# Base weights staged in the attention's operand room, under a newly planned order of instructions: a four-layer block on one core

## The chip, the cores and the metric

The kernel runs on one core of a Trainium2 chip. The metric is the device time of one execution in microseconds, as a median over several runs. The core has five engines that each take their instructions strictly in order: PE (matmul), DVE (vector), ACT (activation), POOL (general purpose), and SP, which issues all DMA transfers of this kernel.

## The reference

The input is x, 32 batches of 128 positions x 1024 channels in float32, and a context of the same shape. Four layers follow each other, each added to its input after a layer norm:

```
x = x + autocorrelation(norm(x), ctx, ctx)     # 8 heads; circular correlation by FFT over the 128
                                               # positions, top 9 lags per channel, softmax, gather
x = x + lora_moe(norm(x), W_base, ...)         # 1024x1024 base product + 8 experts of rank 16, top 2
x = x + windowed_attention(norm(x), ctx, ...)  # channels = the 128 rows, T = 1024, 8 heads, window 16
x = x + lora_moe4(norm(x), A, B, Wr)           # 4 experts of rank 16, top 2
```

The batches are independent of each other.

## The kernel before

Each batch is a 128 x 1024 tile in two halves of 512 columns. `load_batch` loads ctx and x (four DMAs of 256 KB) and splits the scaled ctx into two f16 pieces (high and low; products of two such pairs are taken as three f16 matmuls, `three`). `autocorr` works on one half: `spectrum` multiplies ctx by Fourier matrices and completes the result by two small SBUF-to-SBUF copies on SP (`u<-u`), `cross` multiplies spectra, the stage "top" finds nine lags on DVE, "wt" turns the weights, "inv" goes back. `ffn0` is the base product with its gate, `attention` the windowed attention, `ffn1` the last layer, whose input is turned by DMA transposes (`turn`).

In `attention`, the queries of one half are spread block-diagonally over `qbd` (8 DMAs, one for each head) and the values, written to DRAM (`vd`) before, over `vbd` (4 DMAs). Each is a fixed SBUF tile of 16 KB per partition; only its diagonal blocks are written, so the rest has to be zero from the start. Both are zeroed in the set-up by one POOL memset each (`keep`, L470 and L471).

All other large values live in 49 general slots, `u`, of 128 x 512 float32 each. `prep_ffn` (L542, stage "ws") prepares the weights once: it loads the base weights by 16 DMAs of 256 KB into 16 `u` slots (L552 to L557), takes their largest absolute value on DVE (`wmx`), and after the scale is known makes two f16 pieces of each (`wsp`) on ACT with DVE or POOL; only then the slots are free.

The order of all instructions is worked out on the host before the kernel is emitted. `Planner` records every operation with an estimated duration (`_cost`) and simulates the five engines: whenever one is free it takes, of the operations that are ready, the one with the lowest priority number, if its slots can be had.

```
prio = lambda o: (period * max(o.batch, 0) - o.tail - bias.get(o.stage, 0.0) - bias.get(o.stage + "/" + o.eng, 0.0), o.index)
```

Here `o.tail` is the longest chain of work behind the operation within its batch, `period` is the configuration's T, and the biases (in us) are set for each stage and each stage on an engine. `win` limits how many batches are in flight; `margin`, `su`, `sp`, `ru` and `rp` rule when an operation must leave slots to older ones. `phases` is a list of such sets, each valid from the simulated time `at`. The last entry of `slack` is added to every DMA's duration after the set-up. For a DMA, `op.dur` is the time to landing and `op.cold` how long it occupies SP. The emitted program follows this order on each engine; the trace therefore gives L364 (the emitting line) for almost all instructions, and groups are told apart by their tiles.

Of the kernel before, what the change touches and what calls it, by code (L numbers as in the profile page):

```python
# [12 lines left out]
F32 = mybir.dt.float32  # L13
F32R = mybir.dt.float32r
F16 = mybir.dt.float16
# [7 lines left out]
S = 128  # L23
D = 1024
HALF = 512
EPS = 1e-5
NEG = -3.0e38
TINY = 1e-30
CFG = {'nu': 49, 'en': 'G', 'cl': 'G', 'xl': 'G', 'sm': 'V', 'sw': 'A', 'wg': 'VG', 'q0': 'G', 'ns': 28, 'nt': 48, 'plan': {'phases': [{'at': 0.0, 'T': 20.35, 'margin': 52, 'win': 6, 'su': 75, 'sp': 99, 'ru': 1, 'rp': 0, 'bias': {'kv': -28.7, 'load': 5.3, 'S': -3.8, 'gate': 75.2, 'ffn1': 5.8, 'q': -6.6, 'top': 0.3, 'PV': 0.0, 'inv': 4.8, 'wt': 98.4, 'spec': 6.9, 'wo': 95.5, 'ws': -11.6, 'base': 1.1, 'ffn0': 85.5, 'corr': 4.1, 'setup': -12.4, 'S/Pool': 23.1, 'kv/PE': -6.8, 'kv/Pool': 1.8, 'gate/Activation': -32.5, 'ffn1/Pool': 15.3, 'q/DVE': 34.4, 'q/Activation': 38.2, 'q/Pool': 8.2, 'ffn0/Pool': 52.9, 'setup/PE': -21.7, 'corr/Pool': -8.1, 'gate/DVE': -34.8, 'setup/SP': 26.1, 'corr/Activation': -7.8, 'corr/PE': 3.9, 'wo/DVE': -60.5, 'setup/DVE': 3.5, 'wt/DVE': 1.1, 'load/SP': -11.1, 'spec/SP': -32.0, 'base/DVE': -1.8, 'ws/Activation': -3.7, 'load/PE': 12.0, 'inv/DVE': 3.1, 'load/Activation': -1.9, 'load/Pool': -12.1, 'ws/Pool': -68.6, 'gate/PE': 6.2, 'ws/SP': -23.3, 'PV/Activation': 35.6, 'ffn1/PE': -3.5, 'ws/PE': -45.6, 'inv/Pool': 4.0, 'corr/DVE': 7.5, 'ffn1/SP': 70.1, 'setup/Pool': -26.5, 'top/DVE': 6.4, 'setup/Activation': -2.6, 'top/Pool': 106.8, 'ffn1/Activation': 35.0, 'spec/Activation': 16.1, 'wt/Activation': 35.3, 'ffn0/PE': 3.2, 'q/SP': 5.5, 'q/PE': 0.6, 'ffn0/Activation': -36.7, 'ws/DVE': 17.5, 'top/Activation': 22.8, 'ffn0/DVE': -21.6, 'inv/Activation': 3.1, 'load/DVE': 8.9, 'ffn1/DVE': 62.8, 'inv/PE': 0.0, 'wo/PE': -38.0, 'PV/DVE': 46.6, 'PV/PE': -2.9, 'S/Activation': 6.7, 'wt/PE': 28.9, 'kv/DVE': 19.9, 'S/DVE': 2.0, 'kv/Activation': -7.2, 'kv/SP': 29.4, 'S/PE': -0.3, 'base/PE': -0.9, 'spec/PE': 0.3, 'PV/Pool': 49.6}}], 'slack': [1.0, 0, 292.364]}}
NTOP = int(2 * math.log(S))  # L30
X_SC = 2.0 ** 10
W_SC = 2.0 ** 14
# [72 lines left out]
class Planner:  # L105
# [72 lines left out]
    def _cost(self, op, method, v, kw):  # L178
        size = lambda x: int(np.prod(x.shape[1:]))
        eng, out = op.eng, v["out"]  # L180
        n = size(out)
        src = next((v[k] for k in ("in_", "in0", "1", "in_values") if k in v), out)
        psum = any(x.proto.space == PSUM for x in v.values())
        nsc = sum(tuple(x.shape[1:]) == (1,) for k, x in v.items() if k in ("scale", "bias", "scalar", "scalar1", "scalar2", "2", "3"))
        if eng == "PE":
            rhs = v["rhs"] if "rhs" in v else v["2"]
            n = size(rhs)
            if method == "transpose":
                warm, cold, cols = 107.0, 213.0, 256.0
            elif rhs.proto.dtype == F32:  # L190
                warm, cold, cols = max(222.0 if n > 64 else 140.0, n / 0.6 + 10), max(214.0, n / 0.3), 4.0 * n
            else:
                warm, cold, cols = max(24.8, n / 2.4 + 2.5), max(26.7, n / 1.2), n
                if rhs.proto.dtype == F32R:
                    warm, cold = max(107.0, warm), max(214.0, cold)
            op.dur += warm
            op.cold += cold
            op.cols += cols * src.shape[0] / 128
            return
        if eng == "Activation":  # L200
            op.dur += (n + (61 if src.proto.space == PSUM else 112)) / 1.2 + 94 * (nsc + ("accum_out" in v))
            if src.region()[0] != out.region()[0]:
                op.dur += 127.0
            elif out.proto.ap[-1][0] > 1:
                op.dur += 0.2 * n
        elif eng == "DVE":
            n = max(n, size(src))
            two = method in ("tensor_copy", "tensor_scalar", "memset") and not psum and n > 64
            op.dur += 6 * n / 0.96 + 67 if method == "reciprocal" else (n * (0.5 if two else 1.0) + 64 + 59 * nsc) / 0.96
            op.dur += 70.0 * ("accum_out" in v) + {"match_replace": 67.0, "transpose": 25.0}.get(method, 0.0)  # L210
        elif eng == "Pool":
            small = mybir.dt.size(out.proto.dtype) == 2
            if method == "memset":
                op.dur += 40.0 + (0.85 if small else 0.2) * n
            else:
                rate = (2.8 if small else 1.2) if method == "tensor_scalar" else 1.88 if small else 2.1
                if any(x.proto.ap[-1][0] == 0 for x in v.values()) and n > 128:
                    rate = 1.67
                op.dur += 530.0 if kw.get("op") == ALU.pow else 150.0 + rate * n
        else:  # L220
            run = out.proto.ap[-1][1] * mybir.dt.size(out.proto.dtype)
            dram = any(x.tile is None for x in v.values())
            op.dur += (3200.0 if dram else 2900.0 if run > 128 else 3500.0) + out.shape[0] * n * mybir.dt.size(out.proto.dtype) / 360.0

            op.cold = 450.0 if dram else 720.0 if run > 128 else 840.0
            if kw.get("transpose"):
                op.dur, op.cold = 4400.0, 1430.0

# [147 lines left out]
def mk_kernel(ctx: ExitStack, tc: tile.TileContext, T: dict, out: bass.AP):  # L376
# [8 lines left out]
    def slot(name, shape, dt=F32):  # L385
        return cp.tile(shape, dt, tag=name, name=name)

    slots = {
        "u": [slot(f"u{i}", [128, HALF]) for i in range(CFG["nu"])],
        "p": [pp.tile([128, HALF], F32, tag=f"p{i}", name=f"p{i}") for i in range(8)],  # L390
        "m": [slot(f"m{i}", [128, 128]) for i in range(6)],
        "s": [slot(f"s{i}", [128, 16]) for i in range(CFG["ns"])],
        "t": [slot(f"t{i}", [128, 4]) for i in range(CFG["nt"])],
        "r": [slot(f"r{i}", [128, 128], F32R) for i in range(6)],
    }
    P = Planner(slots)
    V, A, G, PE, SP = (P.engine(n, e) for n, e in zip(
        ("DVE", "Activation", "Pool", "PE", "SP"), (nc.vector, nc.scalar, nc.gpsimd, nc.tensor, nc.sync)))

    def U():  # L400
        return P.tile("u")

    def B():
        return P.tile("p")

    def M():
        return P.tile("m")
# [52 lines left out]
    def keep(name, shape, dt, fill, eng=G):  # L460
        t = P.fixed(slot(name, shape, dt))
        eng.memset(t if dt == F32 else t.bitcast(F32), fill)
        return t
# [3 lines left out]
    tl8, tl4 = ([keep(f"tl{e}_{i}", [128, 8], F32, NEG) for i in range(2)] for e in (8, 4))  # L467
    k16 = keep("k16", [128, 2, D + 16], F16, 0.0)

    qbd = keep("qbd", [128, 2, 32, 128], F16, 0.0)  # L470
    vbd = keep("vbd", [128, 32, 128, 2], F16, 0.0)  # L471


    wst, woT, wb = U(), const("woT", [128, 128]), load("wb")
# [46 lines left out]
    for src, sc, dst in ((wq, sq, None), (wk, rsc[:, 0:1], wk16), (wv, rsc[:, 1:2], wv16)):  # L521
        t, p = M(), B()
# [19 lines left out]
    def prep_ffn():  # L542
# [3 lines left out]
        def load_ar(name, i, w, rows):  # L546
            t = U()[:, 0 : rows * w].rearrange("p (k n) -> p k n", n=w)
            SP.dma_start(out=t, in_=T[name][i * rows * 128 : (i + 1) * rows * 128].rearrange("(k p) n -> p k n", p=128))
            return t


        wb = []  # L552
        for k in range(16):
            t = U()
            SP.dma_start(out=t, in_=T["wbT"][k // 2 * 128 : (k // 2 + 1) * 128, k % 2 * HALF : (k % 2 + 1) * HALF])
            absmax(mx[:, k : k + 1], t)
            wb.append(t)  # L557
        for i in range(4):
            t = load_ar("ar8T", i, 136, 2)
            absmax(mx[:, 16 + i : 17 + i], t[:, :, 0:128], AX.XY)  # L560
            absmax(mx[:, 20 + i : 21 + i], t[:, :, 128:136], AX.XY)
        for i in range(2):
            t = load_ar("ar4T", i, 68, 4)
# [30 lines left out]
        for i in range(4):  # L594
            t = load_ar("ar8T", i, 136, 2)
            for lo, hi, c in ((0, 128, 1), (128, 136, 2)):
                pieces([wsp[:, r, 2 * i : 2 * i + 2, D + lo : D + hi] for r in range(2)], t[:, :, lo:hi], c)
        for k in range(16):
            lo = k % 2 * HALF
            pieces([wsp[:, r, k // 2, lo : lo + HALF] for r in range(2)], wb[k], 0, CFG["wg"][k % len(CFG["wg"])])  # L600
        for i in range(2):
            t = load_ar("ar4T", i, 68, 4)
            for lo, hi, c in ((0, 64, 3), (64, 68, 4)):
                pieces([ar4[:, r, 4 * i : 4 * i + 4, lo:hi] for r in range(2)], t[:, :, lo:hi], c)
        for g in range(2):
            t, sl = U(), slice(g * HALF, (g + 1) * HALF)
# [3 lines left out]
        for g in range(2):  # L610
            t, r, sl = U(), U(), slice(g * HALF, (g + 1) * HALF)
# [5 lines left out]

    prep_ffn()
    P.behind = ()


    def ln_first(src):
# [82 lines left out]
    def load_batch(b):  # L705
# [17 lines left out]
        for g in range(2):  # L723
            if CFG["cl"] == "G":
                A.activation(c16[g][:, 0], c[g], AF.Copy, scale=sc)
# [28 lines left out]
    def autocorr(b, hf, normalise, x, c16, ksc, sums):  # L754
# [3 lines left out]
        q, q16, p = normalise(hf), pair(U()), B()  # L758
        split(q16[:, 0], q16[:, 1], q, G if CFG["q0"] == "G" else V)
        three(p, wdft[:, 0], q16)  # L760
# [333 lines left out]
```

## Time and profile before

| | |
|---|---|
| median of 3 runs | 1609.07 us (1606.35 to 1609.52) |
| profiled execution | 1606.64 us, span 1604.9 us |
| mean granted PE clock | 0.966 |
| PE, DVE, ACT, POOL busy | 94%, 89%, 89%, 85% of the span |
| DMA engines, share of the span | 61.3% (queue of SP) |
| DMA traffic | 179.62 MB, mean 112 GB/s |

The times of engines overlap. Slices of the span are 40 us; in the lines quoted below, `u<-in_ctx` means that a general slot is written from the input ctx, `x` with a number counts instructions, and in square brackets stands how long the engine idled before and what released it.

### The profile page before, as it was taken

What the parts mean: (1) busy time and instruction counts of PE and PEld (TensorE: products, weight loads), DVE (VectorE), ACT (ScalarE), POOL (GpSimd) and SP (SyncE); (2) the same over time, 40 slices, a digit from 0 to 9 for tenths busy, and PEclk for the clock granted to TensorE, in tenths of its full rate; (3) what the DMA queues carried; (4) which work ended last, traced back from release to release, by engine and by line L of the source; (5) the groups of instructions that cost most, each with busy time, mean ns of one, the idle gap of its engine ahead of it and who ended that gap; (6) DMA issues with size and microseconds to landing.
All of it is one profiled execution on the core that took longest, in us unless ns stands there. A gap on an engine that the chain in (4) does not pass through costs nothing.

```text
span 1604.9 us, 52637 instructions
## 1 busy us (share of the span) xinstructions
PE 1504.2 (94%) x19469; PEld 1005.0 (63%) x19469; DVE 1420.7 (89%) x4922; ACT 1420.5 (89%) x2833; POOL 1358.0 (85%) x1569
## 2 busy tenths in 40 slices
PE   3589999999999999999999999999999999999954
PEld 1246666766676666666666666666666666766642
DVE  6878999999999999999999999999999999989753
ACT  5788999999999999999999999999999999998642
POOL 5778988998888899888888998888889988898742
PEclk7799999999999999999999999999999999999975
DMA  8325566666656666566566666657666566666562
GB/s 252 105 75 82 87 111 127 118 113 125 109 105 115 119 120 123 113 127 101 103 126 117 118 119 121 125 98 110 114 127 120 110 128 106 102 96 93 85 78 54
DMA packets 957058, 179.62 MB, mean 112 GB/s; under 512 B 877360, under 2 KB 912960, under 8 KB 956800
## 3 DMA queue, kind: packets, MB, share of 16 engines
q1 hardware_dynamic: 956800, 176.25, 61.3%
q8 instruction: 154, 2.52, 0.6%
q14 instruction: 104, 0.85, 0.2%
HBM read 75.36 MB, written 33.82 MB: 68 GB/s over the span
## 4 chain that ended last, share of the span: by engine, by line
PE 52%; ACT 25%; DVE 9%; DMA 5%; issue 5%; SPq 2%; POOL 1%; ACTq 0%; POOLq 0%; DVEq 0%
PE p L364 52%; ACT u L364 24%; DVE u L364 7%; DMA vbd<-vd 3%; SPq L364 2%; DMA u<-in_x 1%; POOL u L364 1%; ACT k L364 1%; DVE t L364 1%; DMA u<-u 1%; DMA vd<-u 0%; DVE wsp L364 0%; DMA u<-in_wbT 0%; DVE wmx L364 0%; DMA u<-in_wa 0%
## 5 line engine op out<-in xcount | busy, mean ns | idle before, releaser
L364 POOL TENSOR_TENSOR u<-u,u 128x512 f16<-128x512 f32 (+1 forms) x704 | 844.6, 1227 | 56.4 <-ACT u L364 51.7
L364 PE MATMUL p<-wsp,u 128*128 128x512 f16 (+1 forms) x2304 | 398.1, 329 | 2.6 <-ACT u L364 1.4
L364 PEld LDWEIGHTS <-u 128*128 128x128 f16 x3840 | 271.2, 99 | 187.7 <-DMA u<-u 13.6
L364 ACT ACTIVATE u<-p,t 64x512 f32<-64x512 f32 (+3 forms) x512 | 316.8, 648 | 22.2 <-PE p L364 12.4
L364 ACT ACTIVATE u<-u,t 128x512 f32<-128x512 f32 (+1 forms) x448 | 314.8, 723 | 22.7 <-DVE t L364 14.1
L364 ACT ACTIVATE u<-p 64x512 f32<-64x512 f32 (+1 forms) x512 | 299.7, 592 | 36.9 <-PE p L364 29.7
L364 DVE SCALAR_TENSOR_TENSOR u<-p,u 128x512 f32<-128x512 f32 (+1 forms) x384 | 255.6, 678 | 30.2 <-ACT u L364 19.1
L364 PE MATMUL p<-u,ch 128*128 128x512 f16 x960 | 244.3, 385 | 2.7 <-DVE u L364 1.7
L364 DVE SCALAR_TENSOR_TENSOR u<-p,t,u 128x512 f16<-128x512 f32 (+1 forms) x256 | 157.8, 626 | 63.5 <-ACT u L364 62.7
L364 ACT ACTIVATE u<-u,t,t 128x512 f32<-128x512 f32 (+1 forms) x256 | 192.8, 829 | 4.9 <-POOL t L364 3.9
L364 PEld LDWEIGHTS <-vbd 128*128 128x128 f16 x6144 | 161.8, 97 | 45.0 <-issue 44.7
L364 PEld LDWEIGHTS <-qbd 128*128 128x128 f16 x6144 | 171.0, 96 | 25.1 <-issue 1.9
L364 PE MATMUL p<-u,vbd 128*128 128x32 f16 x6144 | 165.7, 177 | 18.6 <-ACT u L364 12.1
L364 PE MATMUL p<-k,qbd 128*128 128x32 f16 x6144 | 174.7, 176 | 1.0 <-DMA vd<-u 1.0
L364 PEld LDWEIGHTS <-ch 128*128 128x128 f16 x960 | 93.0, 102 | 129.4 <-issue 52.7
L364 ACT ACTIVATE u<-u 128x512 f16<-128x512 f32 x194 | 119.5, 639 | 54.5 <-DVE u L364 54.3
L364 POOL TENSOR_TENSOR u<-u,t 128x512 f32<-128x512 f32 x64 | 65.5, 1043 | 81.0 <-DVE t L364 78.1
L364 POOL TENSOR_TENSOR u<-u,s 128x512 f32<-128x512 f32 x128 | 131.7, 1049 | 0.5
L364 PE MATMUL p<-u,cf 128*128 128x512 f32 x256 | 123.9, 604 | 1.2 <-POOL u L364 0.8
L364 POOL TENSOR_TENSOR t<-t,mhalf 128x1 f32<-128x1 f32 x128 | 72.4, 565 | 46.0 <-DVE t L364 45.6
L364 DVE STREAM_TRANSPOSE u<-u 128x512 f32<-128x512 f32 x128 | 89.8, 703 | 9.7 <-POOL u L364 9.2
L364 PE MATMUL p<-ident,u 128*128 128x128 f32 x512 | 82.2, 286 | 11.3 <-POOL u L364 5.4
(163 smaller groups left out, 2661.5 us busy)
## 6 DMA issues: line engine op xcount, KB each, us to landing
vbd<-vd SPq DMA_DIRECT2D x256, 128.0 KB
u<-u SPq DMA_DIRECT2D x192, 128.0 KB
u<-in_ctx SPq DMA_DIRECT2D x64, 256.0 KB
u<-in_x SPq DMA_DIRECT2D x64, 256.0 KB
vd<-u SPq DMA_DIRECT2D x64, 256.0 KB
qbd<-u SPq DMA_DIRECT2D x512, 32.0 KB
out<-u SPq DMA_DIRECT2D x64, 256.0 KB
u<-u SPq DMA_DIRECT2D x64, 126.0 KB
```

The source lines that it names most:

```text
L364: fn(*[f(a) for a in args], **{k: f(a) for k, a in kw.items()})
```

## The change

The two fixed tiles `qbd` and `vbd` are no longer zeroed in the set-up. The 16 loads of the base weights go into them instead of into 16 `u` slots (8 into each, seen as float32), and both are zeroed by POOL memsets after `prep_ffn` has been recorded; the planner's dependences put each memset behind the last use of the weights in its tile and ahead of the first attention operand. In `_cost`, a transfer from or to a DRAM tensor of the interface occupies SP for its bytes at 290 GB/s, at least 450 ns, instead of for 450 ns. The configuration of the planner has new numbers everywhere, and two phases instead of one. Values still go through DRAM, and the inputs of `ffn1` are still turned by DMA.

The core of the diff (the configuration is cut; every bias differs, only some are shown, and lines of it are wrapped):

```
-'phases': [{'at': 0.0, 'T': 20.35, 'margin': 52, 'win': 6, 'su': 75, 'sp': 99, 'ru': 1, 'rp': 0,
-  'bias': {'kv': -28.7, 'load': 5.3, 'S': -3.8, 'gate': 75.2, 'q': -6.6, 'ws': -11.6, 'corr': 4.1,
...
-           'ws/Pool': -68.6, 'ws/DVE': 17.5, 'setup/Activation': -2.6, 'gate/Activation': -32.5,
...
-'slack': [1.0, 0, 292.364]
+'phases': [{'at': 0.0, 'T': 22.27, 'margin': 31, 'win': 6, 'su': 61, 'sp': 4, 'ru': 1, 'rp': 0,
+  'bias': {'kv': -16.7, 'load': 3.8, 'S': -2.0, 'gate': 82.5, 'q': -25.3, 'ws': -13.3, 'corr': -2.3,
...
+           'ws/Pool': -95.6, 'ws/DVE': -9.2, 'setup/Activation': -39.1, 'gate/Activation': 11.7,
...
+          {'at': 1463.0, 'T': 18.19, 'margin': 252, 'win': 4, 'su': 125, 'sp': 2, 'ru': 4, 'rp': 2,
+  'bias': {'kv': -13.7, 'load': -32.2, 'S': -28.6, 'gate': 151.3, 'q': 25.4, 'ws': -29.9, 'corr': 37.0,
...
+'slack': [1.0, 0, 910.686]

-            op.cold = 450.0 if dram else 720.0 if run > 128 else 840.0
+            op.cold = max(450.0, out.shape[0] * n * mybir.dt.size(out.proto.dtype) / 290.0) if dram else 720.0 if run > 128 else 840.0

-    qbd = keep("qbd", [128, 2, 32, 128], F16, 0.0)
-    vbd = keep("vbd", [128, 32, 128, 2], F16, 0.0)
+    qbd = P.fixed(slot("qbd", [128, 2, 32, 128], F16))
+    vbd = P.fixed(slot("vbd", [128, 32, 128, 2], F16))

+        flat = [qbd.bitcast(F32).rearrange("p r b n -> p (r b n)"), vbd.bitcast(F32).rearrange("p b n r -> p (b n r)")]
         wb = []
         for k in range(16):
-            t = U()
+            t = flat[k // 8][:, k % 8 * HALF : (k % 8 + 1) * HALF]
             SP.dma_start(out=t, in_=T["wbT"][k // 2 * 128 : (k // 2 + 1) * 128, k % 2 * HALF : (k % 2 + 1) * HALF])

     prep_ffn()
     P.behind = ()
+    for t in (qbd, vbd):
+        G.memset(t.bitcast(F32), 0.0)
```

More of the change, by code (lines that the diff above doesn't have):

```diff
@@ L28 @@
 TINY = 1e-30
-CFG = {'nu': 49, 'en': 'G', 'cl': 'G', 'xl': 'G', 'sm': 'V', 'sw': 'A', 'wg': 'VG', 'q0': 'G', 'ns': 28, 'nt': 48, 'plan': {'phases': [{'at': 0.0, 'T': 20.35, 'margin': 52, 'win': 6, 'su': 75, 'sp': 99, 'ru': 1, 'rp': 0, 'bias': {'kv': -28.7, 'load': 5.3, 'S': -3.8, 'gate': 75.2, 'ffn1': 5.8, 'q': -6.6, 'top': 0.3, 'PV': 0.0, 'inv': 4.8, 'wt': 98.4, 'spec': 6.9, 'wo': 95.5, 'ws': -11.6, 'base': 1.1, 'ffn0': 85.5, 'corr': 4.1, 'setup': -12.4, 'S/Pool': 23.1, 'kv/PE': -6.8, 'kv/Pool': 1.8, 'gate/Activation': -32.5, 'ffn1/Pool': 15.3, 'q/DVE': 34.4, 'q/Activation': 38.2, 'q/Pool': 8.2, 'ffn0/Pool': 52.9, 'setup/PE': -21.7, 'corr/Pool': -8.1, 'gate/DVE': -34.8, 'setup/SP': 26.1, 'corr/Activation': -7.8, 'corr/PE': 3.9, 'wo/DVE': -60.5, 'setup/DVE': 3.5, 'wt/DVE': 1.1, 'load/SP': -11.1, 'spec/SP': -32.0, 'base/DVE': -1.8, 'ws/Activation': -3.7, 'load/PE': 12.0, 'inv/DVE': 3.1, 'load/Activation': -1.9, 'load/Pool': -12.1, 'ws/Pool': -68.6, 'gate/PE': 6.2, 'ws/SP': -23.3, 'PV/Activation': 35.6, 'ffn1/PE': -3.5, 'ws/PE': -45.6, 'inv/Pool': 4.0, 'corr/DVE': 7.5, 'ffn1/SP': 70.1, 'setup/Pool': -26.5, 'top/DVE': 6.4, 'setup/Activation': -2.6, 'top/Pool': 106.8, 'ffn1/Activation': 35.0, 'spec/Activation': 16.1, 'wt/Activation': 35.3, 'ffn0/PE': 3.2, 'q/SP': 5.5, 'q/PE': 0.6, 'ffn0/Activation': -36.7, 'ws/DVE': 17.5, 'top/Activation': 22.8, 'ffn0/DVE': -21.6, 'inv/Activation': 3.1, 'load/DVE': 8.9, 'ffn1/DVE': 62.8, 'inv/PE': 0.0, 'wo/PE': -38.0, 'PV/DVE': 46.6, 'PV/PE': -2.9, 'S/Activation': 6.7, 'wt/PE': 28.9, 'kv/DVE': 19.9, 'S/DVE': 2.0, 'kv/Activation': -7.2, 'kv/SP': 29.4, 'S/PE': -0.3, 'base/PE': -0.9, 'spec/PE': 0.3, 'PV/Pool': 49.6}}], 'slack': [1.0, 0, 292.364]}}
@@ new lines @@
+CFG = {'nu': 49, 'en': 'G', 'cl': 'G', 'xl': 'G', 'sm': 'V', 'sw': 'A', 'wg': 'VG', 'q0': 'G', 'ns': 28, 'nt': 48, 'plan': {'phases': [{'at': 0.0, 'T': 22.27, 'margin': 31, 'win': 6, 'su': 61, 'sp': 4, 'ru': 1, 'rp': 0, 'bias': {'kv': -16.7, 'load': 3.8, 'S': -2.0, 'gate': 82.5, 'ffn1': 3.4, 'q': -25.3, 'top': 12.8, 'PV': -0.7, 'inv': 7.1, 'wt': 82.5, 'spec': 6.5, 'wo': 65.9, 'ws': -13.3, 'base': 0.6, 'ffn0': 76.5, 'corr': -2.3, 'setup': -7.5, 'S/Pool': 11.5, 'kv/PE': 5.0, 'kv/Pool': -6.7, 'gate/Activation': 11.7, 'ffn1/Pool': 7.1, 'q/DVE': 37.7, 'q/Activation': 40.4, 'q/Pool': 46.5, 'ffn0/Pool': 70.6, 'setup/PE': -40.9, 'corr/Pool': 1.4, 'gate/DVE': -43.9, 'setup/SP': 42.4, 'corr/Activation': -4.5, 'corr/PE': 15.7, 'wo/DVE': -61.5, 'setup/DVE': -3.1, 'wt/DVE': 8.6, 'load/SP': 2.6, 'spec/SP': -38.3, 'base/DVE': 9.3, 'ws/Activation': -1.4, 'load/PE': 19.4, 'inv/DVE': 10.4, 'load/Activation': -6.2, 'load/Pool': -24.4, 'ws/Pool': -95.6, 'gate/PE': 8.2, 'ws/SP': -4.3, 'PV/Activation': 24.0, 'ffn1/PE': -7.0, 'ws/PE': -41.8, 'inv/Pool': 8.6, 'corr/DVE': 10.7, 'ffn1/SP': 85.1, 'setup/Pool': -58.3, 'top/DVE': 0.1, 'setup/Activation': -39.1, 'top/Pool': 112.3, 'ffn1/Activation': 20.6, 'spec/Activation': 22.7, 'wt/Activation': 16.0, 'ffn0/PE': 16.7, 'q/SP': -3.4, 'q/PE': -2.5, 'ffn0/Activation': -44.6, 'ws/DVE': -9.2, 'top/Activation': 22.0, 'ffn0/DVE': -48.1, 'inv/Activation': 12.8, 'load/DVE': 21.9, 'ffn1/DVE': 30.9, 'inv/PE': -0.5, 'wo/PE': -19.7, 'PV/DVE': 35.3, 'PV/PE': -3.7, 'S/Activation': -1.5, 'wt/PE': 4.2, 'kv/DVE': 18.4, 'S/DVE': 0.9, 'kv/Activation': 25.2, 'kv/SP': 27.8, 'S/PE': 23.0, 'base/PE': -1.4, 'spec/PE': 0.7, 'PV/Pool': 17.0}}, {'at': 1463.0, 'T': 18.19, 'margin': 252, 'win': 4, 'su': 125, 'sp': 2, 'ru': 4, 'rp': 2, 'bias': {'kv': -13.7, 'load': -32.2, 'S': -28.6, 'gate': 151.3, 'ffn1': -46.4, 'q': 25.4, 'top': 6.0, 'PV': 14.5, 'inv': 3.8, 'wt': 45.5, 'spec': -0.3, 'wo': 77.1, 'ws': -29.9, 'base': 18.5, 'ffn0': 105.1, 'corr': 37.0, 'setup': -2.8, 'S/Pool': -51.7, 'kv/PE': 11.3, 'kv/Pool': -15.5, 'gate/Activation': 62.0, 'ffn1/Pool': -2.3, 'q/DVE': 37.9, 'q/Activation': 5.0, 'q/Pool': -19.9, 'ffn0/Pool': 81.8, 'setup/PE': -95.4, 'corr/Pool': -11.4, 'gate/DVE': -76.4, 'setup/SP': 30.3, 'corr/Activation': -7.9, 'corr/PE': 48.2, 'wo/DVE': -73.1, 'setup/DVE': -30.9, 'wt/DVE': 5.2, 'load/SP': 1.0, 'spec/SP': -24.4, 'base/DVE': 6.9, 'ws/Activation': 9.2, 'load/PE': 14.3, 'inv/DVE': 1.0, 'load/Activation': 6.5, 'load/Pool': -39.4, 'ws/Pool': -95.1, 'gate/PE': 6.0, 'ws/SP': -68.8, 'PV/Activation': 22.0, 'ffn1/PE': -41.9, 'ws/PE': -65.8, 'inv/Pool': 10.0, 'corr/DVE': -6.3, 'ffn1/SP': 99.7, 'setup/Pool': -64.1, 'top/DVE': 10.2, 'setup/Activation': -70.7, 'top/Pool': 159.7, 'ffn1/Activation': -54.8, 'spec/Activation': 47.8, 'wt/Activation': 16.1, 'ffn0/PE': -11.7, 'q/SP': 6.7, 'q/PE': -10.2, 'ffn0/Activation': 0.6, 'ws/DVE': -4.6, 'top/Activation': 20.9, 'ffn0/DVE': -52.3, 'inv/Activation': 15.1, 'load/DVE': 9.7, 'ffn1/DVE': 31.3, 'inv/PE': 6.1, 'wo/PE': -11.5, 'PV/DVE': 53.2, 'PV/PE': -0.8, 'S/Activation': -15.2, 'wt/PE': -70.6, 'kv/DVE': 42.6, 'S/DVE': 29.1, 'kv/Activation': -21.1, 'kv/SP': 74.3, 'S/PE': 38.4, 'base/PE': -27.2, 'spec/PE': 16.9, 'PV/Pool': 39.6}}], 'slack': [1.0, 0, 910.686]}}
```

## The prediction
> **What bounds the kernel now.** I read the page's first two parts first.
>
> ```profile
> span 1604.9 us, 52637 instructions
> PE 1504.2 (94%) x19469; PEld 1005.0 (63%) x19469; DVE 1420.7 (89%) x4922; ACT 1420.5 (89%) x2833; POOL 1358.0 (85%) x1569
> ...
> PE   3589999999999999999999999999999999999954
> ...
> PEclk7799999999999999999999999999999999999975
> ```
>
> One slice is 40 us. PE is full but for the first three slices and the last two, so I asked for the busy time of each engine in five stretches (columns: length, then PE, PEld, DVE, ACT, POOL busy with counts, granted clock, DMA share, GB/s).
>
> ```profile
> 0.00:30.00 30.00, 7.76 (x22) 3.20 (x22) 16.89 (x44) 17.30 (x28) 17.48 (x30) 0.85 0.94 302
> 30.00:60.00 30.00, 12.11 (x46) 8.98 (x47) 29.95 (x127) 16.68 (x35) 17.38 (x18) 0.56 0.45 114
> 60.00:130.00 70.00, 55.07 (x281) 29.52 (x279) 52.55 (x169) 63.08 (x122) 55.76 (x57) 0.89 0.31 76
> 130.00:1520.00 1390.00, 1385.01 (x18320) 931.78 (x18318) 1282.82 (x4479) 1295.81 (x2597) 1238.73 (x1430) 1.00 0.64 112
> 1520.00:1604.90 84.90, 44.27 (x807) 31.51 (x804) 38.47 (x106) 27.63 (x53) 28.69 (x37) 0.68 0.48 66
> ```
>
> Between 130 and 1520 us PE is busy for 99.6% at full clock: no order of the same instructions can shorten that stretch by more than its 5 us of idle time. The chain of waits in order of time shows its beat: the same 24.1 us piece of PE work returns every 46.1 us, one batch.
>
> ```profile
> 357.39 24.10 PE p L364 x252
> ...
> 403.52 24.10 PE p L364 x252
> ...
> 449.64 24.10 PE p L364 x252
> ```
>
> So 32 batches hold 32 x 46.13 = 1476 us of PE work, and the other 129 us of the span are head and tail. PE idles 130 - 74.9 = 55 us in the head and 84.9 - 44.3 = 41 us in the tail; the rest is set-up work and matmuls at half clock. In the head the limit moves: to 30 us nobody is full, from 30 to 60 DVE is (29.95 of 30: the largest elements of the base weights, the weight pieces and the top-k of the first batches together), from 60 to 130 ACT is (63.08 of 70). The timeline of SP's queue in the head (start, length, what it issues), one line of PE's, and one of the waits (total us, times, longest):
>
> ```profile
> 10.81 9.64 SPq L364 DMA_DIRECT2D u<-in_wbT  x14
> 20.85 2.99 SPq L364 DMA_DIRECT2D u<-u  x4
> ...
> 67.53 1.63 SPq L364 DMA_DIRECT2D u<-in_ctx  x2
> ```
> ```profile
> 30.03 1.22 PE L364 MATMUL p<-cf,u 128*128 128x128 f32 x4 [10.89 <-POOL u L364]
> ```
> ```profile
> DVE u L364 <- DMA u<-u: 3.7, 1, 3.7
> ```
>
> Two batches are loaded by 10.8 us; then the 16 base-weight tiles take 16 of the 49 general slots, and the third batch's ctx is asked for only at 67.5 us, when weight pieces are giving slots back.
>
> **The change, part by part.** The sum is made against the profiled execution, 1606.64 us with its span of 1604.9; the median of the runs is 1609.07, 2.4 more, and is added at the end.
>
> *Sixteen slots freed in the head.* What can use them is a third batch before 60 us. ACT idles 13.3 us between 30 and 60, then is the limit for 70 us, so ACT work brought forward comes off the limit. From the groups of the first 130 us, a batch's ACT work up to its first top-k is 4 scalings of ctx at 711 ns, 4 spectrum evictions at 591, 2 normalisations at 806, 2 splits at 618 and 4 cross evictions at 691: 2.8 + 2.4 + 1.6 + 1.2 + 2.8 = 10.8 us. It fits the 13.3. It needs of DVE 2 reductions at 678, 2 statistics at 680 and 2 products at 683: 4.1 us in the stretch where DVE is full, which pushes the weights back by as much. So between 10.8 and 10.8 - 4.1 = 6.7; the middle, 8.7 us saved. The lower bound for the whole term is zero, if DVE is what PE waits for all along (a rival below).
>
> *Loads costed by their bytes.* The planner charged SP 450 ns for any DRAM transfer; a 256 KB load now stands at 904 ns. The trace shows SP at 9.64 / 14 = 0.69 us for each, and the four small copies of the first spectrum issued behind them land only after 6.23 us (the chain's DMA piece at 21.51); the vbd loads of 128 KB each take 3.3 to 3.5 us in the middle of the chain. A plan that knows this can put the copies first: 6.2 - 3.4 = 2.8 us, bounded by the 3.7 us for which DVE waited there and by zero. I take 2.8. The freed loads need nothing else: SP is past the weights at 24.8 us.
>
> *The two memsets.* They leave the first 10 us, where they hide nothing (POOL's next real work waits for ACT at 11.77), and come back behind the last weight piece and ahead of the first loads of the attention operands (qbd at 121.8, vbd at 133.0 us).
>
> ```profile
> L364 POOL MEMSET qbd<- x1: 3511/3511/3511, 1.6 to 1.6; 128x4096 f32 x1
> L364 POOL MEMSET vbd<- x1: 3515/3515/3515, 5.9 to 5.9; 128x4096 f32 x1
> ```
>
> That is 7.03 us of POOL among the 70 us in which it idles 14.2, but the planner prices each at 40 + 0.2 x 4096 = 859 ns, so 5.3 us come unplanned, and whatever stands behind them in POOL's queue (the low halves of splits, the cross products that PE and DVE wait for) is late by up to that. Their cover is that ACT, not POOL, is the limit; without it they cost 7.0. Bounds 0 and 7.0; I take 2. The last pieces finish at 99 us here, 22 us before the first qbd load, so the new wait (attention of batch 0 on memset on pieces) costs nothing unless the pieces slip by 15 us. The other side of it: the slow DVE piece groups show DVE held up next to POOL (906 ns median for the weight pieces with two SBUF inputs, one of ar at 4254, against 683 ns for products that read PSUM). The Trainium skill (SBUF — State Buffer, the section on engine ports) says that such DVE instructions contend with a GpSimd instruction that reads SBUF and not with one that only writes, while a DVE copy or scalar operation in a 2-port mode is blocked for a GpSimd instruction's whole length. By it a memset could hold a small DVE operation for 3.5 us, and two of them would bring the term to its upper end, 7.0 instead of 2.
>
> *The tail's own phase.* From the planner's 1463 us on another set of priorities rules. The last batches' attention halves go through one qbd, refilled by 8 loads. The queue's timeline and POOL's show what an order could win:
>
> ```profile
> 1552.32 4.63 SPq L364 DMA_DIRECT2D qbd<-u  x6
> 1557.28 3.19 SPq L364 DMA_TRANSPOSE u<-u  x2
> 1560.52 1.33 SPq L364 DMA_DIRECT2D qbd<-u  x2
> ```
> ```profile
> 1572.12 0.25 POOL L364 TENSOR_SCALAR s<-s 128x16 f32<-128x16 f32 x1 [8.60 <-DVE s L364]
> ```
>
> Two transposes of another batch stand inside the last refill, 3.2 us, and a stall of 8.6 follows. But the last batch's own serial chain, from vd at 1527 to the end, stays. I take 4 saved, near the 3.2; bounds 12 saved (3.2 + 8.6) and 8 lost (a stall as long as that one more).
>
> *The middle.* Every bias is new, and DMA landings are planned 0.62 us longer (911 against 292 ns). The floor is 46.13 per batch, so it can only lose. In one period of the chain (265.13 to 311.27) ACT is busy 43.46 of 46.14 us and DVE 42.90, so up to 2.7 us of new waits per batch are hidden. The worst periods here exceed the beat by 1.3 and 3.3 us (from 1187.40 to 1234.82 and from 1373.21 to 1422.64). I take 3 us lost, one such period; bounds 0 and 24 (30 x 0.8, worked out in rival b).
>
> Sum: 1606.6 - 8.7 - 2.8 + 2 - 4 + 3 = 1596.1; on the median, 2.4 more: 1598.5 us. A measurement of this kernel tells some 0.2% (3.2 us) from no change, so the boundaries are 1605.9 and 1612.3.
>
> **Rivals.** (a) *DVE is the wall.* In 30 to 60 DVE has 0.05 us left, and a third batch's work there, whole autocorrelations included, only delays the weights; the copies' 2.8 go the same way. For it: those 29.95 us. Against: ACT alone is the limit for the next 70. Then 1606.6 + 2 - 4 + 3 + 2.4 = 1610.
>
> (b) *ACT becomes the bound in the middle.* It has the least spare time, 2.7 us per batch. If the new order puts an ACT instruction ahead of its input so that ACT waits 3.5 us per batch (the length of one vbd landing, 3.3 to 3.5 in the chain), 0.8 us per batch come through on 30 batches, 24 us: 1598.5 - 3 + 24 = 1619.5. It decides the sign from (8.7 + 2.8 - 2 + 4) / 30 = 0.45 us per batch. For it: all orders here are strict per engine, and the tightly repeating beat was found with biases that are all replaced. Against: landings are now planned more cautiously, and in the order of before PE waited for almost nothing with the same spare time.
>
> (c) *Both ends come out at their bounds*, 10.8 + 3.7 in the head and 12 in the tail, no memset cost and no loss in the middle: 1606.6 - 26.5 + 2.4 = 1582.
>
> **How the numbers follow.** Forecast 0.44 (1588 to 1605, all faster); (a) 0.13, of which 0.03 faster, 0.07 same, 0.03 slower; (b) 0.35, slower, between 1613 and 1636; (c) 0.08. Faster 0.44 + 0.03 + 0.08 = 0.55, same 0.07, slower 0.38. The range must reach into (b): from 1581 to 1630, where (b) has 1.2 us per batch.
>
> **What would show it.** In the stretches after: ACT busier than 16.7 us between 30 and 60, ctx of the third batch asked for before 60 us, PE full before 120 us instead of 130: the head is right. The spectrum's copies landing in some 3 us: the load costing is right. The two memsets of 3.5 us between the last piece and the first qbd load, with PE's waits for POOL there no longer than before: their price is right. Less than 80 us from the end of full PE to the end of the span: the tail. A beat over 46.6 us in the chain, or PE under 99% between 130 and 1500, is (b), and makes the prediction wrong; a head that still fills at 130 us is (a).

## The result and the profile after

The changed kernel takes 1593.78 us (median of 4 runs, 1590.91 to 1595.45), the kernel before 1607.95 us in the same comparison (4 runs). The ratio is 0.991, with a 95% interval from 0.9891 to 0.9929: 14 us faster. A second comparison on another occasion gave 0.9912 (0.9898 to 0.9925). The profiled execution took 1590.91 us with a span of 1589.1 us, 15.8 less than the span before.

The page of the changed kernel, first two parts (slices of 39.7 us):

```profile
span 1589.1 us, 52604 instructions
PE 1506.3 (95%) x19469; PEld 997.5 (63%) x19469; DVE 1409.1 (89%) x4922; ACT 1413.1 (89%) x2833; POOL 1361.2 (86%) x1569
...
PE   4689999999999999999999999999999999999964
...
PEclk8799999999999999999999999999999999999985
```

PE's busy time is that of before to 2 us; it is spread over less time. The busy times by stretch (length, PE, PEld, DVE, ACT, POOL, granted clock, DMA share, GB/s) say where:

```profile
0.00:30.00 30.00, 14.80 (x55) 8.19 (x56) 22.18 (x98) 22.70 (x40) 18.50 (x36) 0.89 0.82 274
30.00:60.00 30.00, 19.96 (x60) 8.56 (x59) 27.22 (x88) 27.41 (x50) 21.54 (x23) 0.78 0.69 185
60.00:130.00 70.00, 57.53 (x418) 35.16 (x417) 60.52 (x209) 61.64 (x130) 58.26 (x57) 0.89 0.38 83
130.00:1520.00 1390.00, 1380.90 (x18289) 921.45 (x18288) 1266.91 (x4447) 1278.39 (x2571) 1239.51 (x1424) 1.00 0.67 112
1520.00:1589.10 69.10, 33.08 (x653) 24.13 (x651) 32.25 (x84) 22.93 (x43) 23.36 (x30) 0.66 0.40 64
```

In the first 60 us PE does 60 + 55 = 115 matmuls against 68 before, and from 60 to 130 us 418 against 281. ACT's hole between 30 and 60 us is filled (27.41 instead of 16.68).

Busy time hides the half clock, so one more measure is used from here on, PE's **lost time**: each matmul counts with the median distance from its start to the next matmul's start that matmuls of its operands and shape have in the kernel before between 300 and 1300 us, the counts of all matmuls that started before a time t are summed, and the sum is taken from t. All 32 batches come to 1453.4 us in every kernel; what a span holds beyond that is lost.

| lost by (us) | 30 | 60 | 130 | 190 | 1440 | end |
|---|---|---|---|---|---|---|
| before | 25.8 | 50.5 | 74.9 | 77.4 | 98.9 | 151.4 |
| after | 21.7 | 39.3 | 59.5 | 62.2 | 86.4 | 135.7 |
| after, second profile | 22.2 | 39.5 | 60.1 | 62.9 | 85.9 | 135.6 |

So the head (to 190 us) gives 15.2 us, the middle takes back 2.7 (24.2 lost instead of 21.5), and the tail gives 3.2 (49.3 instead of 52.5): 15.7 of the span's 15.8. The split depends a little on the measure: with medians by shape alone it reads 16.3, -2.7 and 2.2, so it is good to about 1 us.

### The profile page after: what moved, and what is told of

The parts are those of the page before. It is cut to its first block, busy times and chain, and to the rows that moved or that the text cites. A ratio compares the mean times of both kernels' runs of the same rounds, so it can differ in the third digit from the quotient of the medians.

```text
span 1589.1 us, 52604 instructions
## 1 busy us (share of the span) xinstructions
PE 1506.3 (95%) x19469; PEld 997.5 (63%) x19469; DVE 1409.1 (89%) x4922; ACT 1413.1 (89%) x2833; POOL 1361.2 (86%) x1569
## 4 chain that ended last, share of the span: by engine, by line
PE 54%; ACT 21%; DVE 8%; POOL 7%; issue 5%; DMA 3%; SPq 1%; POOLq 0%; ACTq 0%; DVEq 0%
PE p L364 54%; ACT u L364 19%; POOL u L364 6%; DVE u L364 5%; DMA u<-u 2%; ACT p L364 1%; SPq L364 1%; DVE s L364 1%; DMA vbd<-vd 1%; DVE mm L364 1%; DVE t L364 1%; ACT k L364 1%; DMA u<-in_x 1%; ACT m L364 0%; POOL t L364 0%
## 5 line engine op out<-in xcount | busy, mean ns | idle before, releaser
L364 POOL TENSOR_TENSOR u<-u,u 128x512 f32<-128x512 f32 (+1 forms) x704 | 849.2, 1230 | 103.3 <-ACT u L364 92.2
L364 PE MATMUL p<-wsp,u 128*128 128x512 f16 (+1 forms) x2304 | 402.3, 329 | 4.5 <-DVE u L364 4.4
L364 ACT ACTIVATE u<-u,t,t 128x512 f32<-128x512 f32 (+1 forms) x256 | 196.6, 811 | 9.9 <-POOL t L364 5.8
L364 PEld LDWEIGHTS <-vbd 128*128 128x128 f16 x6144 | 166.2, 97 | 45.4 <-issue 38.8
L364 PEld LDWEIGHTS <-qbd 128*128 128x128 f16 x6144 | 170.1, 96 | 25.4 <-issue 7.3
L364 DVE SCALAR_TENSOR_TENSOR u<-p,t,u 128x256 f32<-128x256 f32 (+1 forms) x256 | 155.5, 621 | 30.9 <-ACT u L364 26.3
L364 PE MATMUL p<-u,vbd 128*128 128x32 f16 x6144 | 168.4, 177 | 15.2 <-ACT u L364 10.2
L364 PEld LDWEIGHTS <-ch 128*128 128x128 f16 x960 | 87.1, 99 | 121.6 <-issue 47.4
L364 ACT ACTIVATE u<-u 128x512 f16<-128x512 f32 (+1 forms) x194 | 117.5, 624 | 27.1 <-DVE u L364 22.8
L364 PE MATMUL p<-u,cf 128*128 128x512 f32 x256 | 131.8, 612 | 3.3 <-POOL u L364 3.3
L364 DVE TENSOR_REDUCE s<-p 128x16 f32<-128x512 f32 x128 | 87.2, 681 | 10.3 <-PE p L364 9.0
L364 DVE TENSOR_REDUCE s<-u 128x16 f32<-128x512 f32 x128 | 85.5, 678 | 4.5 <-ACT u L364 3.7
```

Of the source, the lines that this page charges most:

```text
L364: fn(*[f(a) for a in args], **{k: f(a) for k, a in kw.items()})
```

## The experiments

All were timed against the kernel before. Most keep the order of the changed kernel, or of before, and edit the planned order just ahead of its emission, since planning again would change everything at once.

**1. The yardstick.**

> The changed kernel once more, unedited, as the yardstick for the three others on the same chip. Both theories: 0.991 of before (0.989 to 0.993), a span near 1589 us, and the same places in the head: PE busy about 92 us of the first 130.

Measured: 1592.08 us, 0.9912 (0.9898 to 0.9925), span 1589.0 us, PE busy 92.3 us to 130. As expected; differences below are to this run where it was on the same chip.

**2. Loads ahead of the copies.**

```
+    dma = [o for o in P.order if o.what == "dma_start"]
+    early = [o for o in dma if o.stage == "ws"][1:15]
+    rest = [o for o in P.order if o not in early]
+    at = rest.index(next(o for o in dma if o.stage == "spec"))
+    P.order = rest[:at] + early + rest[at:]
```

> The order of the changed kernel, but on SP's queue 14 of the 16 loads of the base weights are issued ahead of the four copies of the first spectrum, as in the kernel before. Theory 1 (the prediction's term: copies behind the loads land 2.8 us later and PE waits): the copies land 5 to 7 us after their issue, PE idles some 10 us between 20 and 30 us again, and the total is 2 to 4 us more than the changed kernel. Theory 2 (DVE or ACT is the limit of the head, and weights that come earlier make up for it): within 1 us, although the copies land late.

Measured: 1598.69 us, 0.9957 (0.9944 to 0.9971), 6.6 us slower than the yardstick, more than theory 1 gave. SP's queue in the changed kernel (start, length, issue), and the same queue in this experiment:

```profile
10.44 0.43 SPq L364 DMA_DIRECT2D qbd<-in_wbT  x1
14.78 3.07 SPq L364 DMA_DIRECT2D u<-u  x4
17.91 3.30 SPq L364 DMA_DIRECT2D qbd<-in_wbT  x7
21.25 5.24 SPq L364 DMA_DIRECT2D vbd<-in_wbT  x7
```
```profile
10.72 5.14 SPq L364 DMA_DIRECT2D qbd<-in_wbT  x8
16.24 4.37 SPq L364 DMA_DIRECT2D vbd<-in_wbT  x7
21.02 3.03 SPq L364 DMA_DIRECT2D u<-u  x4
```

The four copies are issued 6.2 us later, and PE, which in the changed kernel goes on at 21.9 us, waits until 30 (timelines of PE, changed kernel first; in brackets the idle time before and what ended it):

```profile
21.90 1.16 PE L364 MATMUL p<-cf,u 128*128 128x128 f32 x8 [1.80 <-POOL u L364]
```
```profile
29.98 2.08 PE L364 MATMUL p<-cf,u 128*128 128x128 f32 x8 [9.79 <-POOL u L364]
```

Little of this shows at once: lost time is some 3 us higher at 30 us and 2 us higher at 60 (41.4 against 39.5). The rest comes out later, 7 us at 90 us (60.5 against 53.6), and stays: 69.6 against 62.9 at 190 us. DVE carries it there. From 15 to 30 us DVE is busy for 7.13 us here and for 14.11 in the yardstick. From 60 to 79 us it is nearly full in both (18.43 and 18.54 of 19 us), and the next long run of matmuls, which waits for DVE, starts 6.0 us later (timelines of PE, yardstick first):

```profile
79.11 6.40 PE L364 MATMUL p<-wsp,u 128*128 128x512 f16 x30 [1.05 <-DVE u L364]
```
```profile
85.15 7.19 PE L364 MATMUL p<-wsp,u 128*128 128x512 f16 x30 [1.03 <-DVE u L364]
```

The weights, which are issued earlier here, buy nothing back.

**3. The same repair in the order of before.**

```
+    late = [o for o in dma if o.stage == "ws"][8:14]
+    rest = [o for o in P.order if o not in late]
+    at = rest.index([o for o in dma if o.stage == "spec"][3]) + 1
+    P.order = rest[:at] + late + rest[at:]
```

> The kernel before in its own order, but on SP's queue the last 6 of the 14 base-weight loads that stand ahead of the first spectrum's four copies are issued behind them. Theory 1 (the copies' place is worth some 7 us, as it was in the changed kernel): PE starts again before 27 us instead of at 30, and the total is 3 to 7 us less than before. Theory 2 (in the order of before DVE is full from 30 to 60 us anyway, and later weights cancel the gain): within 1.5 us of before.

Measured: 1606.09 us, 1.0 (0.9991 to 1.0008). The repair was only in part one: with 8 loads still ahead, the chain shows the copies landing 6.14 us after 17.15, and PE going on at 28.45 us, 1.6 earlier than before, not before 27. Those 1.6 us vanish at once: DVE is full from 30 to 60 us in this kernel too, and lost time at 60 is 50.3 against 50.5. A full repair, with all 14 loads behind the copies, was not run in this order.

```profile
30.00:60.00 30.00, 11.58 (x42) 7.58 (x42) 29.97 (x130) 16.68 (x35) 16.34 (x18) 0.50 0.44 117
```

**4. The room undone, order kept.** The changed kernel with the weights in `u` slots and the zeroing in the set-up; `RANK` holds each operation's place in the changed kernel's order.

```
-                prio = lambda o: (period * max(o.batch, 0) - o.tail - bias.get(...) - bias.get(...), o.index)
+                prio = lambda o: (int(RANK[o.index]), o.index)
-            t = flat[k // 8][:, k % 8 * HALF : (k % 8 + 1) * HALF]
+            t = U()
```

> The changed kernel without the room: the base weights are loaded into 16 general slots and both fixed tiles are zeroed in the set-up. The planner's priority is the place of each operation in the changed kernel's order, so it keeps that order where slots allow it. Theory 1 (the 16 slots carry the rest of the head's gain): from 30 to 60 us ACT is busy 16 to 20 us instead of 27, PE is full at 125 us or later, and PE's lost time at 190 us is back at 70 or more (62 in the changed kernel, 77 in before), even though the two memsets no longer stand on POOL's chain. Theory 2 (priorities and the copies' place do it alone): the head is like that of the changed kernel or better by the 7 us of the memsets. The total can be higher in either case, since behind the head the order is no longer a tuned one; the head decides.

Measured: 1610.82 us, 1.0031 (1.0021 to 1.0041). The head answers for theory 1: the copies are early here too (issued at 14.55 us) and lost time at 30 us is the changed kernel's, 22.2; but then slots run out, ACT's hole is back, and lost time at 190 us is 75.2.

```profile
30.00:60.00 30.00, 14.00 (x61) 7.66 (x62) 26.03 (x90) 17.57 (x41) 11.93 (x19) 0.58 0.47 133
60.00:130.00 70.00, 53.22 (x267) 29.46 (x266) 57.97 (x198) 68.01 (x133) 59.94 (x59) 0.85 0.44 106
```

The room is worth 75.2 - 62.9 = 12.3 us to this order, with the memsets' place included. This order was made for the room; an order tuned without it, but with the new costs and priorities, was not tried, so how much planning alone could have won stays open.

**5. The room alone**, in the order of before (`RANK` from before, weights in the fixed tiles, old costs and phase).

> The room alone: the kernel before with the base weights loaded into the fixed tiles and the memsets behind them, old DMA costs and old phase; the planner's priority is the place of each operation in the order of before, so the order stays but for what the 16 free slots let it bring forward. The copies stay behind the loads. Theory 1 (free slots are enough): ACT is busier than 22 us from 30 to 60, PE's lost time at 190 us falls from 77 to 72 or less although the memsets now cost up to 7. Theory 2 (free slots are worth something only with copies ahead of the loads and priorities that use them): ACT stays at 16 to 19 us there and the lost time is 77 or more. The total is likely above that of before in either case, since the order behind the head is no longer a tuned one.

Measured: 1644.9 us, 1.024 (1.0225 to 1.0255); what it loses behind the head is an order that is no longer a tuned one, as expected. In the head it is between the theories: the free slots are used (the next ctx is asked for at 32 us instead of 67.5, ACT is busy 22.46 us from 30 to 60), and lost time at 60 us is 3.4 lower than before, 47.1. At 165 us it is still some 1.5 us below before, but at 190 us it is 79.2, 1.8 above. In this order the slots, with the two memsets that they bring, move work and do not shorten the head.

**6. The memsets doubled.**

```
+    for o in P.order:
+        if o.stage == "ws" and o.what == "memset":
+            o.calls = o.calls * 2
```

> The order of the changed kernel is kept; each of the two memsets is emitted twice, 7.0 us more of POOL at the same places (81 and 108 us). Theory 1 (the chain of the changed kernel runs over POOL from 88 to 112 us, so POOL is the limit there and the memsets are paid in full): 5 to 7 us slower than the changed kernel, PE's last long wait ends at 117 to 120 instead of 113 us. Theory 2 (the price of 2 us in the prediction: ACT is the limit and covers POOL): 0 to 2 us slower.

Measured: 1599.83 us, 0.9956 (0.9944 to 0.9969), 7.7 us slower than the yardstick for 7.0 us of memsets. The chain of waits from 111 us on (start, length, what):

```profile
111.40 3.46 POOL vbd L364
...
114.91 3.51 POOL vbd L364
118.42 0.52 POOL t L364
...
119.23 0.82 ACT u L364
...
120.10 4.91 PE p L364 x29
```

Both copies of vbd's memset stand on it, and PE is full only behind them.

**7. vbd zeroed by DVE.** One line: the call of the second memset becomes `nc.vector.memset`.

> The order of the changed kernel is kept; the memset of vbd is issued by DVE instead of POOL, at the same place of the order, where DVE idles 3.4 us (from 111.7 to 115.0). Theory 1 (POOL is the limit): the layer norm and the cross product behind the memset on POOL come 3.5 us earlier, 2 to 3.5 us faster than the changed kernel. Theory 2 (POOL is covered): no difference, within 1 us. A third way: the memset takes DVE more than its idle time, and it is 1 to 3 us slower.

Measured: 1594.12 us, 0.9927 (0.9913 to 0.994), 2.0 slower than the yardstick, with intervals that overlap. The memset takes DVE 3.47 us and starts at 108.36, in the middle of a top-k, not in the hole that I had seen behind it; in the changed kernel's trace that hole is put down to ACT (3.35 us at 115.03). Lost time at 190 us is 63.3 against 62.9, so the head gained nothing from a POOL without this memset, as theory 2 had it. The 2.0 us lie behind the head (25.8 lost from 190 to 1440 us against 23.0), where nothing was edited and other profiles of this order lose as much; so the third way is not shown either.

**8. Zeroing by DMA.** Both tiles, or one of them, are filled by SP from the part of k16 that is still zero.

```
+    zero = k16.bitcast(F32)[:, 0, 0:HALF].unsqueeze(1).broadcast_to([128, 8, HALF])
...
+    o.calls = [(nc.sync.dma_start, (), dict(out=flat, in_=zero))]
```

> The order of the changed kernel, but both fixed tiles are zeroed by two DMAs of SP (2 MB each, read from the part of k16 that is still zero) behind the last weight piece instead of by POOL. Theory 1 (the memsets are paid in full on POOL's chain, as the doubled ones were, and SP and the DMA engines are idle there: 11% to 23% busy from 80 to 100 us): 5 to 7 us faster than the changed kernel, 0.987 of before, PE's lost time at 190 us 55 to 58 instead of 63. Theory 2 (the 4 MB stand in the way of the first attention's transfers from 99 us on): between 2 us faster and 4 us slower.

> As zero_dma, but only qbd is zeroed by a DMA (2 MB, about 7 us of the DMA engines from 81 us); vbd's memset stays on POOL. Theory 1 (each memset costs its 3.5 us on POOL's chain, and in zero_dma the gain went into the ar4 weights that landed 10.1 us after their issue, behind 4 MB): the ar4 weights land within some 4 us of their issue at 88 us, PE's lost time at 190 us is 59 to 61 instead of 63, 2 to 4 us faster than the changed kernel. Theory 2 (POOL's chain from 88 to 112 is held by something else, so that only added POOL time shows): within 1.5 us.

> As zero_dma, but only vbd is zeroed by a DMA, from 86 to 88 us on; qbd's memset stays on POOL at 81 us. Theory 1 (the vbd memset stands on the chain with its full 3.44 us): 2 to 4 us faster than the changed kernel, unless the ar4 loads issued right behind it land after 95 us, when ACT needs them: then 0 to 2 us. Theory 2: within 1.5 us.

Measured, as ratios to before: both 0.9903 (0.9887 to 0.992), qbd alone 0.992 (0.9907 to 0.9932), vbd alone 0.991 (0.9896 to 0.9924). None is told apart from the changed kernel's 0.9912. Lost time at 190 us is 62.5, 65.3 and 61.2 against 62.9. With vbd off POOL, the chain goes from POOL to the weights of the last layer, whose load is issued right behind the fill:

```profile
87.15 1.24 POOL bl L364
...
88.40 9.56 DMA u<-in_ar4T
...
97.98 0.51 ACT ar L364
```

The trace of the changed kernel shows no wait for that load; with vbd filled, ACT waits 2.2 us for it. So theory 1 of zero_dma (5 to 7 us) is wrong, and so is that of fill_qbd: the ar4 transfer explains fill_vbd and zero_dma, but with qbd alone filled, the chain still runs over POOL and the vbd memset (3.44 us at 109.65), and PE is full at 114.8 instead of 113.5 us (yardstick). That its head lost 2.4 us more is within what two profiles of one order differ by (last section); that it gained nothing is what counts, and why qbd's memset, too, is replaced by another wait I have not settled.

**9. Without the second phase**, and **10. the second phase under the order of before.** Only `phases` is edited.

> The changed kernel without the second phase: the same order up to the planner's 1463 us, the priorities of the first phase to the end. Theory 1 (the second phase makes the tail's 3 us): 2 to 5 us slower than the changed kernel, all of it behind 1460 us. Theory 2 (the tail is the last batch's chain whatever the priorities): within 1 us.

> The kernel before with the changed kernel's second phase appended to its own first one: the order of before up to the planner's 1463 us, the new tail behind it. Theory 1 (the second phase is good for a tail as such): 2 to 4 us less than before. Theory 2 (a tail's priorities fit only the order they were made with, or do nothing): between 1 us less and 5 us more.

Measured: 1596.47 us without it, 0.9939 (0.9927 to 0.9952), about 4 us slower than the changed kernel; 1606.03 us with it added to before, 0.9999 (0.999 to 1.0008). Lost from 1440 us to the end: 53.1 without it, 49.7 in the yardstick; 51.4 in before with it, 52.5 without. Theory 1 for the changed kernel, theory 2 for before. SP's queue in the tail of the changed kernel, then without the second phase:

```profile
1538.11 6.42 SPq L364 DMA_DIRECT2D qbd<-u  x8
1545.99 2.64 SPq L364 DMA_TRANSPOSE u<-u  x2
1549.68 3.08 SPq L364 DMA_DIRECT2D vbd<-vd  x4
```
```profile
1541.80 4.54 SPq L364 DMA_DIRECT2D qbd<-u  x6
1546.65 2.81 SPq L364 DMA_TRANSPOSE u<-u  x2
1549.52 1.32 SPq L364 DMA_DIRECT2D qbd<-u  x2
1554.40 2.19 SPq L364 DMA_DIRECT2D vbd<-vd  x4
```

The two transposes inside the last refill, which the prediction pointed at in before, are there again in the second list and gone from the first. In before with the second phase they still stand inside the last refill (at 1557.22 and 1559.70 us), and that kernel gains nothing. This fits the prediction's reading; the place of the transposes by itself was not tested.

## Why the prediction was right, point by point

The sign and the place held: 1598.5 us was forecast, 10.6 less than the 1609.07 known then, most of it in the head; 14.2 us less was measured in the comparison. Against the profiled execution the sum said 10.5 less, and 15.7 were measured; nearly all of the difference lies in the head, forecast at 8.7 + 2.8 - 2 = 9.5 us and measured at 15.2. The sum by its terms:

| term | forecast | measured |
|---|---|---|
| slots in the head | -8.7 | -12.3, memsets' place included (experiment 4) |
| copies ahead of the loads | -2.8 | -6.7 of lost time in the head (experiment 2) |
| memsets | +2 | not separated: 7.0 us more of them cost 7.7 us (experiment 6); without them on POOL the lost time is between 1.7 less and 2.4 more (experiments 7 and 8) |
| middle | +3 | +2.7 (lost time, 190 to 1440 us) |
| tail | -4 | -3.2; without the phase 3.4 more is lost (experiment 9) |

The first three were costed apart and cannot be added as measured: they act on one head that gained 15.2 us.

*Slots.* The amount was right and the work was not. I wrote that two batches are loaded by 10.8 us and that a third would use the slots; the timeline has three pairs of ctx loads by then, in both kernels, and the next one, asked for at 67.5 us, is the fourth. In the changed kernel it is asked for at 54.68, late in the stretch. What fills ACT there (27.41 - 16.68 = 10.7 us, where I had 10.8; that the two agree is luck) are batches that had already been loaded. ACT's groups from 30 to 60 us, changed kernel first (busy us, mean ns, then idle before):

```profile
L364 ACT ACTIVATE u<-p,t 64x512 f32<-64x512 f32 (+1 forms) x14 | 9.6, 682 | 0.3
L364 ACT ACTIVATE u<-p 64x512 f32<-64x512 f32 (+1 forms) x14 | 8.3, 592 | 0.3
```
```profile
L364 ACT ACTIVATE u<-p 64x512 f32<-64x512 f32 (+1 forms) x6 | 3.6, 593 | 2.6 <-PE p L364 2.5
```

The first line is 14 spectrum evictions (I had the lengths of the two kinds the other way round, which leaves the sum as it is); 12 of the second line are cross evictions, against 4 of the third. DVE has begun top-k's for four halves by 70 us (16 instructions of MAX8) against two (8). That the loaded batches had lacked slots for their intermediate tiles is what experiment 4 says for the changed order; in the order of before, free slots alone brought ACT only to 22.46 us (experiment 5).

*Copies.* This is the term that was mis-sized: I bounded it by DVE's wait of 3.7 us for the copies. But PE's idle line beside it, 10.89 us, was the better bound. In experiment 2 a wait of 9.79 us comes back, POOL and DVE wait 10.0 and 7.2 us for the copies, and 6.7 us are lost in the end; in the changed kernel no engine's wait in the head is put down to these copies. The 7 us of work that DVE then cannot do between 15 and 30 us are missing when it is full, from 60 to 79 us. In the kernel before, DVE is full already from 30 to 60 us, and 1.6 us of an earlier start were worth nothing (experiment 3), as rival (a) said.

*Memsets.* I took ACT to be the limit from 60 to 130 us, because it was in before. In the changed kernel POOL is, just where the memsets stand: 23.92 us busy of the 24 from 88 to 112, against 15.95 before. The chain of the changed kernel runs over it:

```profile
100.05 3.71 POOL u L364 x3
103.76 1.12 POOL k L364
104.88 1.23 POOL u L364
...
107.80 3.44 POOL vbd L364
```

So the cover that I named is gone, and another 7 us of memsets cost 7.7. Yet the memsets that are there cost little by what takes them away: at most 1.7 us of lost time, for vbd's, and nothing that the times tell. Other waits, for ACT, DVE and the last layer's weights, come right behind POOL. The kernel with the zeroing left out altogether was not timed. The Trainium skill's rule that was weighed there (SBUF — State Buffer, section "Who interferes with whom": a DVE instruction in a 2-port mode is blocked for a GpSimd instruction's whole length when that one came first) was not seen to decide anything: beside qbd's memset (81.1 to 84.6 us) DVE's small TENSOR_SCALARs on `kvs` took 0.26 us, as in the kernel before, and its weight pieces 0.73 to 0.74 us. Whether any of them ran in such a mode the trace does not show.

*Middle and tail.* That the middle came out at 2.7 is luck. I took 3 us as "one such period", but those periods were misread: the row at 1187.40 holds 258 matmuls instead of 252 and is itself 1.30 us longer, which is all of the first excess, and the row at 1422.64 (435 matmuls in full) is not the piece that starts at 1373.21. The tail's 4 was near its measured 3.2, and experiment 9 fits the reason given.

*Rivals.* (a), DVE as the wall, is true of the order of before from 30 to 60 us (29.95 of 30 us). In the changed order it is not gone but displaced: DVE is busy 27.22 us of that stretch, and all 19.00 us from 60 to 79, where the weight pieces now stand; experiment 2 shows PE waiting for it there. Its price was wrong all the same, since the head gained 15.2 us. (b), ACT as the bound of the middle, did not come: ACT is busy 92.0% from 130 to 1520 us and PE 99.3%, and the beat is still PE's. The chain has nearly the same run of work 184.13 us apart, which is 46.03 a batch if it is four batches:

```profile
984.19 101.94 PE p L364 x1354
...
1168.32 102.09 PE p L364 x1354
```

The middle's loss is small but real: 190 to 1440 us loses 24.2, 23.0 and 25.4 us in three profiles of the changed order (after, the yardstick, one_phase), 23.6 to 27.0 in the other six that keep it, and 21.5, 21.3 and 21.2 in three of the order of before (before, copies_first, before_phase2). Which wait makes it is not shown.

*Signs named ahead.* ACT busier than 16.7 us from 30 to 60: yes. The next ctx before 60: yes, at 54.68. PE full before 120: yes, lost time grows only from 59.4 to 59.5 between 120 and 130 us. The copies: nothing in the changed kernel's head waits for them, so their landing does not show. PE's waits for POOL no longer than before: by the letter yes, 1.1 us in the 70 us from 60 to 130 against 2.3; but the chain to PE runs over POOL and vbd's memset and then ACT, so this sign did not test the memsets' price. The tail: the lost time above shows it better than the length I named.

## What to carry to other kernels

Memory freed for a short while is worth what the engines lack at that moment: the same 16 slots gave 12 us to an order made for them, with its small copies ahead of the bulk loads, and nothing net to the order of before; the copies' place gave 7 us with the slots, and half the repair without them gave nothing. So test such edits together and apart, with the order held still, before crediting one of them. When work is moved to an engine that is idle in the old profile, ask which engine will be the limit in the new one: POOL idled 8 of the 24 us from 88 to 112 before, and 0.1 after. And follow a limit that seems to be gone: DVE's full stretch moved from 30-60 to 60-79 us, and that is where late copies came to be paid.

## What the runs showed of the hardware

A memset of 128 x 4096 float32 takes 3.47 us on DVE (vbd_dve) and 3.50 to 3.52 on POOL (before, after), so nothing is won by moving it for speed. A fill of 2 MB from SBUF to SBUF, read 8 times over from one 2 KB row of each partition, is one issue of 0.6 to 0.7 us for SP, but a load of 2 x 136 KB queued behind it lands 9.6 us after its issue (fill_vbd). Two profiles of the same order differ by up to 2.4 us in lost time at 190 us (before and before_phase2, 77.4 and 79.8), so a smaller difference between two single profiles tells nothing.
